# LSTM gates in the order i, f, g, o, with the output gate's columns transposed, summed and put through tanh in a later piece

## The chip, the cores and the metric

The kernel runs on one core of a Trainium2 chip. The metric is the device time of one execution in microseconds (us), less is better. A core has five engines that matter here: TensorE (PE in the profile, PEld for its weight loads) multiplies matrices into PSUM; VectorE (DVE) does elementwise work, sums along a row and transposes of 32x32 blocks; ScalarE (ACT) does tanh and copies; GpSimd (POOL) and SyncE (SP) issue transfers and little else in this kernel. Each engine works through its own list of instructions in order[...].

## The reference, cut to what matters

Four residual layers follow each other over x of shape (4, 1024, 512): a tanh RNN, a state-space layer, an LSTM and an adapted linear layer. The change touches the LSTM alone.

```python
# x = x + RNN(x, cond); x = x + SSM(x, ...); then the LSTM, width 512, 1024 steps, batch 4:
xW = jnp.einsum('ntd,dg->ntg', x, Wx) + b
c0 = jnp.zeros_like(h0)
def step(carry, xw_t):
    prev_h, prev_c = carry
    A = xw_t + prev_h @ Wh                 # (4, 2048): gates i, f, o, g
    i = jax.nn.sigmoid(A[:, 0:Hdim])
    f = jax.nn.sigmoid(A[:, Hdim:2 * Hdim])
    o = jax.nn.sigmoid(A[:, 2 * Hdim:3 * Hdim])
    g = jnp.tanh(A[:, 3 * Hdim:4 * Hdim])
    next_c = f * prev_c + i * g
    next_h = o * jnp.tanh(next_c)
    return ((next_h, next_c), next_h)
_, hs = jax.lax.scan(step, (h0, c0), jnp.swapaxes(xW, 0, 1))
# x = x + hs; then the adapted linear layer
```

Each of the 1024 steps needs the h of the step before, so no two steps of a recurrence can be computed at once. The products i*g and f*c need three gates; the output gate o is needed only when h is formed.

## The kernel before, in words

**Stages.** The sequence is cut into 32 chunks of 32 steps. A loop of passes (`do_pass`, L737) handles one chunk of the LSTM per pass, step by step (L765), and beside each LSTM step one step of the RNN, which runs 56 steps ahead (LEAD). The other layers' work for neighbouring chunks (input projections, the state-space layer, the adapted layer of the last chunk) is a list of jobs, each with a step and a place in it: "pe" after the LSTM's matmuls, "gap" in the middle of VectorE's LSTM work, "end" after the RNN's. In passes -2 and -1 only the RNN and the setup run; there Wh2 is split into three bf16 parts (`split_wh2`, L269), and Wx2, b2 and the adapted layer's weights are made ready. In pass 0 and 1 the adapted layer's matrices are also computed.

**Order.** It is written out by hand: each engine runs its instructions in the order in which the code emits them (manual schedule), and the framework only adds the semaphores that data dependences need.

**One LSTM step.** h is held as three parts of bf16 precision (`split`, L189, twice per half after h itself), so the weights loaded into TensorE are 128x12: three parts of four batch rows. The hidden units are worked in two halves, A and Bh, each of 256 units. `lstm_mm(c, t, kh, mh, ks)` (L359) emits the matmuls that take the h of half kh into the accumulator of half mh (`acc2[mh]`, a PSUM tile of 128x256): for each of two blocks k of 128 units and each of three parts n of Wh2 four matmuls, which write the four 32-row strips of the tile. A step has thus 96 matmuls, 24 groups of four. Their order (L770 to L774): A's h into A (6 groups), first block of A's h into Bh (3), Bh's h into A (6), second block of A's h into Bh (3), Bh's h into Bh (6). After the fifteenth group A's accumulator is complete.

The columns of `acc2` are four gates of 64 columns, in the reference's order i, f, o, g. `Half` (L378) has the steps that follow, for each half: `transpose` (L386, VectorE) turns the accumulator to units by batch, into `tt2`, where `lstm_input` (L375, ScalarE) has laid the input's part beside the three partial results; `sum` (L391) adds the four; `gates` (L398, ScalarE) takes tanh of all gates at once (sigmoid is written as tanh of half the value, and g's weights are doubled); `products` (L402), `cell` (L407), `tanh` (L412, ScalarE), `h` (L415) and `split` twice (L191). The tile `gc` keeps i, f, o, g and, as a fifth block, the cell state that came from the step before. The loop body from L780 interleaves the halves by hand: A's transpose and sum, Bh's transpose, A's gates, products and cell, Bh's sum, A's tanh, h and first split, Bh's gates and products, A's second split, Bh's cell; then the "gap" jobs, the copies of the next input, Bh's tanh, h and splits; then the RNN's transpose (L352), add (L353) and tanh (L356), and the "end" jobs.

The next step's first LSTM matmul reads all three parts of A's h and so waits for A's second split; its tenth group is the first that reads Bh's.

**Gates' places elsewhere.** `wx2` (L164) holds Wx2 as it lies in memory, loaded by four transfers on SP's queue; `b2` (L148) is loaded gate by gate; `split_wh2` writes the columns of gate g; `double_g` (L265) and a job at L670 double the columns and bias of g.

Of the kernel before, what the change touches and what calls it, by code (L numbers as in the profile page):

```python
# [8 lines left out]
F32 = mybir.dt.float32  # L9
BF16 = mybir.dt.bfloat16  # L10
AF = mybir.ActivationFunctionType
ALU = mybir.AluOpType
PSUM = bass.MemoryType.PSUM

P = 128
B, T, D = 4, 1024, 512
KC = D // P
TC = 32
# [4 lines left out]
CT = 32  # L23
TAPS = B
NG = 4 * KC
NS = 64
RANK = 8
WR = 2
W2_BUFS = 4
NP = 3  # L30
# [8 lines left out]
def cond_resid_kernel(ctx: ExitStack, tc: tile.TileContext, a: dict, out: bass.AP):  # L39
# [28 lines left out]
    nc = tc.nc  # L68
    ctx.enter_context(tc.manual_schedule())

    const = ctx.enter_context(tc.tile_pool(name="const", bufs=1))
# [10 lines left out]
    def quads(eng, dst, src):  # L82

        for j in range(4):
            eng.dma_start(out=dst[CT * j : CT * (j + 1)], in_=src[j])

    def load_rows(pool, name, src, n, eng):

        t = pool.tile([P, KC, n], F32, name=name, tag=name)
        quads(eng, t, src.rearrange("(j c q) n -> j q c n", j=4, c=KC))  # L90
        return t
# [21 lines left out]
    gc = [turns(4, f"gc{m}", [P, 5, 2, B]) for m in range(2)]  # L113
    prod = [turns(2, f"prod{m}", [P, 2, 2, B]) for m in range(2)]
# [4 lines left out]
    x1 = state.tile([P, KC, 3 + TC, B], F32, name="x1", tag="x1")  # L119
    s1 = state.tile([NS, B], F32, name="s1", tag="s1")  # L120

# [25 lines left out]
    bo = load_vec(const, "bo", a["bo"].rearrange("j (c q) -> j q c", q=CT).unsqueeze(2), 1, nc.gpsimd)  # L147
    b2 = const.tile([P, 4, KC], F32, name="b2", tag="b2")  # L148
    for g in range(4):
        quads(nc.gpsimd, b2[:, g], a["b2"].rearrange("(g j) (c q) -> g j q c", g=4, q=CT)[g])  # L150

    load_x(1, a["xT"][1])
    load_x(2, a["xT"][2])
# [1 line left out]
    layer = const.tile([P, B, KC, D], F32, name="layer", tag="layer")  # L155
    for c in (1, 0, 2, 3):
        quads(nc.sync, layer[:, c], a["Wh2"].rearrange("(j c q) (g n) -> j c q g n", j=4, c=KC, g=4)[:, c])
    wh2 = [const.tile([P, KC, 4 * D], BF16, name=f"wh2{i}", tag=f"wh2{i}") for i in range(NP)]
# [2 lines left out]
    quads(nc.sync, wp[:, TAPS - 1], a["Wp"].rearrange("(j c q) n -> j q c n", j=4, c=KC))  # L161
    ws = load_rows(const, "ws", a["Ws"], NS, nc.sync)
    wo = load(const, "wo", [NS, D], a["Wo"], nc.sync)
    wx2 = load_rows(const, "wx2", a["Wx2"], 4 * D, nc.sync)  # L164
    w1 = layer[:, 1]

    base = layer[:, B - 1]
# [17 lines left out]
    def upper(x):  # L185

        return x.bitcast(BF16)[..., 1::2]
# [12 lines left out]
    for n in range(1, NP):  # L200
        split(h2[1][:, :, TC - 1], n)
    for m in range(2):
        nc.vector.memset(gc[m][0][:, 4], 0.0)
    nc.vector.memset(x1[:, :, 0:3, :], 0.0)
    nc.vector.memset(s1, 0.0)

# [1 line left out]
    acc2 = [psum.tile([P, 2 * P], F32, name=f"acc2{i}", tag=f"acc2{i}") for i in range(2)]  # L208
# [54 lines left out]
                nc.gpsimd.tensor_scalar(wp[:, tap, k], whole[:, k], condT[:, k, tap : tap + 1], None, ALU.mult)  # L263

    def double_g(k):  # L265
        w = wx2[:, k, 3 * D :]
        nc.scalar.activation(w, w, AF.Copy, scale=2.0)

    def split_wh2(k, g):  # L269

        w, scale, cols = layer[:, k, g], 1.0 if g == 3 else 0.5, slice(g * D, (g + 1) * D)
        part = [x[:, k, cols] for x in wh2]
        left = xw2[1][:, 2 + g % 2].rearrange("p c t b -> p (c t b)")

        def first():
            nc.scalar.activation(part[0], upper(w), AF.Copy, scale=scale)
            nc.vector.scalar_tensor_tensor(left, w, scale, part[0], ALU.mult, ALU.subtract)

        def second():
            nc.scalar.copy(part[1], upper(left))  # L280
            nc.vector.tensor_tensor(part[2], left, part[1], ALU.subtract)

        return first, second
# [72 lines left out]
        nc.scalar.activation(h0[c % 2][:, :, t, :], pre0[t % 2], AF.Tanh)  # L356


    def lstm_mm(c, t, kh, mh, ks=(0, 1)):  # L359


        h = h2[c % 2] if t else h2[(c - 1) % 2]
        for k in (2 * kh + x for x in ks):
            parts = upper(h[:, k, (t - 1) % TC].rearrange("p s b -> p (s b)"))
            for n in range(NP):
                w = wh2[n][:, k].rearrange("p (g n) -> p g n", g=4)
                for j in range(4):
                    n0 = P * j + 2 * CT * mh
                    nc.tensor.matmul(  # L369
                        acc2[mh][CT * j : CT * j + NP * B, :], parts, w[:, :, n0 : n0 + 2 * CT],  # L370
                        start=(k == 0 and n == 0), stop=(k == KC - 1 and n == NP - 1),
                    )

    def lstm_input(c, t, m):
        nc.scalar.copy(tt2[m][t % 2][:, :, :, :B], xw2[c % 2][:, :, 2 * m : 2 * m + 2, t, :])  # L375
# [1 line left out]
    class Half:  # L377


        def __init__(self, c, t, m):  # L380
            self.m, self.tt, self.gc, self.th = m, tt2[m][t % 2], gc[m][t % 4], th2[m][t % 4]
            self.prod, self.c = prod[m][t % 2], gc[m][(t + 1) % 4][:, 4]
            self.out = h2[c % 2][:, 2 * m : 2 * m + 2, t]

        def transpose(self):
            nc.vector.transpose(  # L386
                self.tt[:, :, :, B:].rearrange("p g c b -> p (g c) b"), acc2[self.m]
            )

        def sum(self):  # L390
            nc.vector.tensor_reduce(  # L391
                self.gc[:, :4].rearrange("p g c b -> p (g c) b"),
                self.tt[:, :, :, : (1 + NP) * B].rearrange("p g c (s b) -> p (g c) b s", b=B),
                axis=mybir.AxisListType.X, op=ALU.add,
            )

        def gates(self):
            nc.scalar.activation(self.gc[:, :4], self.gc[:, :4], AF.Tanh, scale=0.5)  # L398

        def products(self):  # L400

            nc.vector.scalar_tensor_tensor(  # L402
                self.prod, self.gc[:, 0:2], 1.0, self.gc[:, 3:5], ALU.add, ALU.mult
            )

        def cell(self):
# [6 lines left out]

        def h(self):
            nc.vector.scalar_tensor_tensor(  # L415
                self.out[:, :, 0], self.gc[:, 2], 1.0, self.th, ALU.add, ALU.mult
            )

        def split(self, n):
# [222 lines left out]
    def at(c, t, f):  # L642
        early.setdefault((c, t), []).append(f)

    def at_step(i, f):

        c, t = divmod(i - LEAD, TC)
        at(c, t, f)
# [18 lines left out]
    at_step(25, adapt_norm)  # L667
    for half in range(2):
        at_step(26 + half, lambda half=half: adapt_bias(half))
    at_step(26, lambda: nc.scalar.activation(b2[:, 3], b2[:, 3], AF.Copy, scale=2.0))  # L670
    for k in range(KC):
        at_step(27 + k, lambda k=k: double_g(k))
    at_step(31, adapt_hidden)
# [12 lines left out]
    for n in range(B * KC):  # L686
        c, t = divmod(24 + 4 * n // 3, TC)
# [49 lines left out]
    def do_pass(c, first=0, src=None, dst=None):  # L737

        lstm = c >= 0
        jobs = []  # L740
        if dst is not None:
            jobs += adapt_jobs(c - 1, dst)
        if -1 <= c < NCHUNK - 1:
            jobs += ssm_jobs(c + 1)
            jobs += input_jobs(
                c + 1, 0, range(25, 29), ((28, "end"), (29, "gap"), (29, "end"), (30, "gap"))
            )
        if src is not None:
            jobs.append((9, "end", lambda: load_x(c + 4, src)))
        if c + 3 < NCHUNK:  # L750
            for m in range(KC):
                mm, end = project0(c + 3, m)
                t = (18, 20, 22, 30)[m]
                jobs += [(t, "pe", mm), (t, "end", end)]
        if lstm:
            jobs += input_jobs(c, 1, range(4), ((3, "end"), (4, "gap"), (4, "end"), (5, "gap")))
            jobs += input_jobs(c, 2, range(4, 8), ((8, "gap"), (8, "end"), (9, "gap"), (9, "end")))
            jobs += input_jobs(c, 3, range(9, 17, 2), ((15, "end"), (16, "gap"), (18, "gap"), (19, "gap")))

        def do(t, place):  # L760
            for slot, where, f in jobs:
                if (slot, where) == (t, place):
                    f()

        for t in range(first, TC):  # L765
            r = divmod(c * TC + t + LEAD, TC)
            rnn = r[0] < NCHUNK
            if lstm:
                A, Bh = Half(c, t, 0), Half(c, t, 1)
                lstm_mm(c, t, 0, 0)  # L770
                lstm_mm(c, t, 0, 1, (0,))
                lstm_mm(c, t, 1, 0)
                lstm_mm(c, t, 0, 1, (1,))
                lstm_mm(c, t, 1, 1)  # L774
            do(t, "pe")
            if rnn:
                rnn_mm(*r)
            if c * TC + t < 8 - TC:
                keep_busy()
            if lstm:  # L780
                A.transpose()
                A.sum()
                Bh.transpose()
                A.gates()
                A.products()
                A.cell()
                Bh.sum()
                A.tanh()
                A.h()
                A.split(1)  # L790
                Bh.gates()
                Bh.products()
                A.split(2)
                Bh.cell()
            do(t, "gap")
            if lstm:
                if (c, t) != (NCHUNK - 1, TC - 1):
                    for m in range(2):
                        lstm_input(c if t + 1 < TC else c + 1, (t + 1) % TC, m)
                Bh.tanh()  # L800
                Bh.h()
                Bh.split(1)
                Bh.split(2)
            if rnn:
                rnn_pre(*r)
                rnn_h(*r)
            do(t, "end")
            for f in early.pop((c, t), ()):
                f()
# [77 lines left out]
```

## Time and profile before

| | us |
|---|---|
| median of 3 runs | 4768.19 (4766.73 to 4770.69) |
| the profiled execution, its own time | 4770.03 |
| its span, first to last instruction | 4768.2 |
| TensorE busy (matmuls) | 4608.4 (97%) |
| TensorE weight loads | 3524.3 (74%) |
| VectorE busy | 3867.3 (81%) |
| ScalarE busy | 1493.9 (31%) |
| first and last transpose of an LSTM accumulator (L386) | 158.2 and 4755.2 |

What lies around the span is 1.8 us. The page's chain of work that ended last is followed back from the last instruction, at each step to what released it. The timeline lists instructions by time: start, duration, engine, line, operation and tiles, and in brackets how long the engine sat idle before it and what ended that. Groups of instructions give the count, the busy time in all, the mean of one in ns, and the idle time before them. Matmuls' ends are modelled: each is drawn with its latency, though four on different strips of PSUM run side by side and the next group starts before the last has ended.

### The profile page before, as it was taken

What the parts mean: (1) busy time and instruction counts of PE and PEld (TensorE: products, weight loads), DVE (VectorE), ACT (ScalarE), POOL (GpSimd) and SP (SyncE); (2) the same over time, 40 slices, a digit from 0 to 9 for tenths busy, and PEclk for the clock granted to TensorE, in tenths of its full rate; (3) what the DMA queues carried; (4) which work ended last, traced back from release to release, by engine and by line L of the source; (5) the groups of instructions that cost most, each with busy time, mean ns of one, the idle gap of its engine ahead of it and who ended that gap; (6) DMA issues with size and microseconds to landing.
All of it is one profiled execution on the core that took longest, in us unless ns stands there. A gap on an engine that the chain in (4) does not pass through costs nothing.

```text
span 4768.2 us, 320158 instructions
## 1 busy us (share of the span) xinstructions
PE 4608.4 (97%) x146784; PEld 3524.3 (74%) x146784; DVE 3867.3 (81%) x18001; ACT 1493.9 (31%) x7645; POOL 45.6 (1%) x80
## 2 busy tenths in 40 slices
PE   7999999999999999999999999999999999999976
PEld 5767777777777777777777777777777777777654
DVE  3688888888888888888888888888888888888876
ACT  2223333333333333333333333333333333333322
POOL 3000000000000000000000000000000000000000
PEclk9999999999999999999999999999999999999999
DMA  6300000000000000000000000000000000000000
GB/s 148 112 13 9 9 7 9 9 7 9 9 7 9 9 7 9 9 7 9 9 7 9 9 7 9 9 7 9 9 7 9 9 7 9 9 5 7 6 5 7
DMA packets 38266, 67.36 MB, mean 14 GB/s; under 512 B 8609, under 2 KB 25505, under 8 KB 35889
## 3 DMA queue, kind: packets, MB, share of 16 engines
q1 hardware_dynamic: 34064, 46.68, 3.6%
q8 instruction: 1147, 18.79, 1.6%
q14 instruction: 207, 1.69, 0.1%
q0 software_dynamic: 1696, 0.19, 0.0%
q10 hardware_dynamic: 1152, 0.01, 0.0%
HBM read 38.34 MB, written 8.39 MB: 10 GB/s over the span
## 4 chain that ended last, share of the span: by engine, by line
PE 94%; DVE 4%; DMA 1%; issue 1%; ACT 0%; SPq 0%; ACTq 0%; DVEq 0%
PE acc L369 59%; PE acc L337 18%; PE proj L318 9%; PE pb L292 3%; PE proj L292 2%; PE ada L703 2%; DVE tt L386 1%; DVE gc L391 1%; DVE h L191 1%; PE ssm_out L292 1%; DMA layer<-in_w_dram 1%; DVE h L415 0%; DVE prod L402 0%; DVE gc L407 0%; PE pl L625 0%
## 5 line engine op out<-in xcount | busy, mean ns | idle before, releaser
L369 PE MATMUL acc<-wh,h 128*12 128x256 bf16 x98304 | 2868.0, 273 | 118.4 <-DVE h L191 115.2
L369 PEld LDWEIGHTS <-h 128*12 128x12 bf16 x98304 | 2262.6, 87 | 676.8 <-DVE h L191 360.6
L386 DVE STREAM_TRANSPOSE tt<-acc 128x256 f32<-128x256 f32 x2048 | 920.9, 450 | 429.2 <-PE acc L369 301.4
L337 PEld LDWEIGHTS acc<-wh,h 128*4 128x4 f32 x32768 | 805.4, 87 | 510.0 <-issue 214.8
L337 PE MATMUL acc<-wh,h 128*4 128x128 f32 x32768 | 1086.1, 273 | 18.1 <-ACT h L356 11.0
L398 ACT ACTIVATE gc<-gc 128x32 f32<-128x32 f32 x2048 | 469.8, 229 | 1279.1 <-DVE gc L391 1192.2
L391 DVE TENSOR_REDUCE gc<-tt 128x32 f32<-128x128 f32 x2048 | 775.4, 379 | 35.3
L191 DVE TENSOR_TENSOR h<-h 128x8 f32<-128x8 f32 (+1 forms) x4098 | 680.5, 166 | 104.8
L412 ACT ACTIVATE th<-gc 128x8 f32<-128x8 f32 x2048 | 427.7, 209 | 830.1 <-DVE gc L407 830.1
L356 ACT ACTIVATE h<-pre 128x16 f32<-128x16 f32 x1024 | 221.2, 216 | 1132.2 <-DVE pre L353 1132.2
L318 PE MATMUL proj<-wx,x 128*32 128x512 f32 x4096 | 529.1, 592 | 1.1 <-DVE x L507 1.1
L415 DVE SCALAR_TENSOR_TENSOR h<-gc,th 128x8 f32<-128x8 f32 x2048 | 341.8, 167 | 144.6 <-ACT th L412 134.7
L407 DVE SCALAR_TENSOR_TENSOR gc<-prod 128x8 f32<-128x8 f32 x2048 | 342.0, 167 | 35.5
L352 DVE STREAM_TRANSPOSE tt<-acc 128x128 f32<-128x128 f32 x1024 | 316.0, 309 | 61.8 <-PE acc L337 61.6
L375 ACT COPY tt<-xw 128x32 f32<-128x32 f32 x2048 | 327.8, 207 | 0.0
L402 DVE SCALAR_TENSOR_TENSOR prod<-gc 128x16 f32<-128x16 f32 x2048 | 314.3, 153 | 0.0
L353 DVE TENSOR_TENSOR pre<-xw,tt 128x16 f32<-128x16 f32 x1024 | 179.3, 175 | 38.0 <-DVE tt L352 0.5
L292 PE MATMUL proj<-xin,wx 128*32 128x128 f32 x4096 | 137.9, 278 | 11.1 <-DMA wx<-in_Wx_dram 11.1
L703 PE MATMUL ada<-layer,x 128*32 128x512 f32 x1024 | 133.9, 599 | 3.0 <-DVE x L696 3.0
L292 PE MATMUL pb<-x,wp 128*32 128x128 f32 x4096 | 134.4, 273 | 0.0
L292 PEld LDWEIGHTS proj<-xin,wx 128*32 128x32 f32 x4096 | 117.5, 112 | 14.9 <-DMA wh<-in_Wh_dram 11.1
L318 PEld LDWEIGHTS proj<-wx,x 128*32 128x32 f32 x4096 | 118.3, 110 | 6.6 <-DVE x L507 1.4
(118 smaller groups left out, 1168.8 us busy)
## 6 DMA issues: line engine op xcount, KB each, us to landing
layer<-in_w2T_dram SPq DMA_DIRECT2D x32, 512.0 KB, 4.5
xin<-in_xT_dram SPq DMA_DIRECT2D x128, 64.0 KB, 2.4
out_dram<-x SPq DMA_DIRECT2D x128, 64.0 KB, 2.0
layer<-in_Wh_dram SPq DMA_DIRECT2D x16, 256.0 KB, 9.9
wx<-in_Wx_dram SPq DMA_DIRECT2D x4, 1024.0 KB, 15.6
wx<-in_Wx_dram SPq DMA_DIRECT2D x4, 256.0 KB, 4.6
wh<-in_Wh_dram SPq DMA_DIRECT2D x4, 256.0 KB, 7.2
layer<-in_w_dram SPq DMA_DIRECT2D x4, 256.0 KB, 23.9
```

Source lines behind the costliest of these rows:

```text
L191: nc.vector.tensor_tensor(h[:, :, n], h[:, :, n - 1], upper(h[:, :, n - 1]), ALU.subtract)
L292: nc.tensor.matmul(dst[CT * j : CT * (j + 1)], columns(j), x, start=first, stop=final)
L318: nc.tensor.matmul(ps[CT * j : CT * (j + 1), :], tok, w[:, j], start=(k == 0), stop=(k == KC - 1))
L337: nc.tensor.matmul(acc0[CT * j : CT * j + B, :], h[:, k, (t - 1) % TC, :], wh0[:, k, j * P : (j + 1) * P], start=(k == 0), stop=(k == KC - 1),
L369: nc.tensor.matmul(acc2[mh][CT * j : CT * j + NP * B, :], parts, w[:, :, n0 : n0 + 2 * CT], start=(k == 0 and n == 0), stop=(k == KC - 1 a ...
L375: nc.scalar.copy(tt2[m][t % 2][:, :, :, :B], xw2[c % 2][:, :, 2 * m : 2 * m + 2, t, :])
L386: nc.vector.transpose(self.tt[:, :, :, B:].rearrange("p g c b -> p (g c) b"), acc2[self.m])
L391: nc.vector.tensor_reduce(self.gc[:, :4].rearrange("p g c b -> p (g c) b"), self.tt[:, :, :, : (1 + NP) * B].rearrange("p g c (s b) -> p ( ...
L398: nc.scalar.activation(self.gc[:, :4], self.gc[:, :4], AF.Tanh, scale=0.5)
L407: nc.vector.scalar_tensor_tensor(self.c, self.prod[:, 1], 0.5, self.prod[:, 0], ALU.mult, ALU.add)
L412: nc.scalar.activation(self.th, self.c, AF.Tanh, scale=0.5)
L415: nc.vector.scalar_tensor_tensor(self.out[:, :, 0], self.gc[:, 2], 1.0, self.th, ALU.add, ALU.mult)
```

## The change

The gates are kept in the order i, f, g, o in all places (`PLACE` maps the old place to the new one): in b2, in the columns of the split Wh2, in Wx2 and in `gc`, where the cell state now lies fourth and the output gate fifth. Wx2's load becomes three slices of columns, each by four transfers. For each half, the transpose, the sum and tanh are each cut in two: the first piece takes i, f and g (192 of the 256 columns, 24 of the 32 gate columns after the sum), the second the output gate (64 and 8). A's second pieces of transpose and sum stand right behind its first; Bh's are spread among A's later steps, and Bh's first transpose now stands between A's products and A's cell. `lstm_mm` takes a list of the six (k, n) groups instead of blocks k, and one group moves: Bh's accumulator gets two groups before Bh's h is read and four after A is complete, instead of three and three.

```diff
+PLACE = (0, 1, 3, 2)
...
-        quads(nc.gpsimd, b2[:, g], a["b2"].rearrange("(g j) (c q) -> g j q c", g=4, q=CT)[g])
+        quads(nc.gpsimd, b2[:, PLACE[g]], a["b2"].rearrange("(g j) (c q) -> g j q c", g=4, q=CT)[g])
...
-    wx2 = load_rows(const, "wx2", a["Wx2"], 4 * D, nc.sync)
+    wx2 = const.tile([P, KC, 4 * D], F32, name="wx2", tag="wx2")
+    for src, dst, n in ((0, 0, 2), (3, 2, 1), (2, 3, 1)):
+        quads(
+            nc.sync, wx2[:, :, dst * D : (dst + n) * D],
+            a["Wx2"].rearrange("(j c q) n -> j q c n", j=4, c=KC)[:, :, :, src * D : (src + n) * D],
+        )
...
-    def lstm_mm(c, t, kh, mh, ks=(0, 1)):
+    def lstm_mm(c, t, kh, mh, parts=range(2 * NP)):
...
+        for x in parts:
+            k, n = 2 * kh + x // NP, x % NP
+            w = wh2[n][:, k].rearrange("p (g n) -> p g n", g=4)
+            for j in range(4):
...
-        def transpose(self):
+        def transpose(self, g0=0, g1=3):
             nc.vector.transpose(
-                self.tt[:, :, :, B:].rearrange("p g c b -> p (g c) b"), acc2[self.m]
-            )
-
-        def sum(self):
+                self.tt[:, g0:g1, :, B:].rearrange("p g c b -> p (g c) b"),
+                acc2[self.m][:, 2 * CT * g0 : 2 * CT * g1],
+            )
+
+        def sum(self, g0=0, g1=3, to=0):
             nc.vector.tensor_reduce(
-                self.gc[:, :4].rearrange("p g c b -> p (g c) b"),
-                self.tt[:, :, :, : (1 + NP) * B].rearrange("p g c (s b) -> p (g c) b s", b=B),
+                self.gc[:, to : to + g1 - g0].rearrange("p g c b -> p (g c) b"),
+                self.tt[:, g0:g1, :, : (1 + NP) * B].rearrange("p g c (s b) -> p (g c) b s", b=B),
                 axis=mybir.AxisListType.X, op=ALU.add,
             )
 
-        def gates(self):
-            nc.scalar.activation(self.gc[:, :4], self.gc[:, :4], AF.Tanh, scale=0.5)
+        def gates(self, g0=0, g1=3):
+            nc.scalar.activation(self.gc[:, g0:g1], self.gc[:, g0:g1], AF.Tanh, scale=0.5)
+
+        def transpose_o(self):
+            self.transpose(3, 4)
+
+        def sum_o(self):
+            self.sum(3, 4, to=4)
+
+        def gate_o(self):
+            self.gates(4, 5)
 
         def products(self):
             nc.vector.scalar_tensor_tensor(
-                self.prod, self.gc[:, 0:2], 1.0, self.gc[:, 3:5], ALU.add, ALU.mult
+                self.prod, self.gc[:, 0:2], 1.0, self.gc[:, 2:4], ALU.add, ALU.mult
             )
...
                 lstm_mm(c, t, 0, 0)
-                lstm_mm(c, t, 0, 1, (0,))
+                lstm_mm(c, t, 0, 1, (0, 1))
                 lstm_mm(c, t, 1, 0)
-                lstm_mm(c, t, 0, 1, (1,))
+                lstm_mm(c, t, 0, 1, (2, 3, 4, 5))
                 lstm_mm(c, t, 1, 1)
...
                 A.transpose()
                 A.sum()
-                Bh.transpose()
+                A.transpose_o()
+                A.sum_o()
                 A.gates()
                 A.products()
+                A.gate_o()
+                Bh.transpose()
                 A.cell()
+                Bh.transpose_o()
+                A.tanh()
                 Bh.sum()
-                A.tanh()
+                Bh.gates()
                 A.h()
+                Bh.sum_o()
                 A.split(1)
-                Bh.gates()
+                Bh.gate_o()
                 Bh.products()
                 A.split(2)
                 Bh.cell()
             do(t, "gap")
```

`h` reads the output gate from `gc[:, 4]` instead of `gc[:, 2]`; `double_g`, `split_wh2` and the job that doubles b2's g use the new places.

More of the change, by code (lines that the diff above doesn't have):

```diff
@@ L202, in cond_resid_kernel @@
     for m in range(2):
-        nc.vector.memset(gc[m][0][:, 4], 0.0)
+        nc.vector.memset(gc[m][0][:, 3], 0.0)
     nc.vector.memset(x1[:, :, 0:3, :], 0.0)
@@ L265, in double_g @@
     def double_g(k):
-        w = wx2[:, k, 3 * D :]
+        w = wx2[:, k, 2 * D : 3 * D]
         nc.scalar.activation(w, w, AF.Copy, scale=2.0)
     def split_wh2(k, g):
-        w, scale, cols = layer[:, k, g], 1.0 if g == 3 else 0.5, slice(g * D, (g + 1) * D)
+        w, scale, cols = layer[:, k, g], 1.0 if g == 3 else 0.5, slice(PLACE[g] * D, (PLACE[g] + 1) * D)
         part = [x[:, k, cols] for x in wh2]
@@ L356, in rnn_h @@
         nc.scalar.activation(h0[c % 2][:, :, t, :], pre0[t % 2], AF.Tanh)
-    def lstm_mm(c, t, kh, mh, ks=(0, 1)):
+    def lstm_mm(c, t, kh, mh, parts=range(2 * NP)):
         h = h2[c % 2] if t else h2[(c - 1) % 2]
[L363 to L371, printed above, removed]
-                    )
+        for x in parts:
+            k, n = 2 * kh + x // NP, x % NP
+            w = wh2[n][:, k].rearrange("p (g n) -> p g n", g=4)
+            for j in range(4):
+                n0 = P * j + 2 * CT * mh
+                nc.tensor.matmul(
+                    acc2[mh][CT * j : CT * j + NP * B, :],
+                    upper(h[:, k, (t - 1) % TC].rearrange("p s b -> p (s b)")), w[:, :, n0 : n0 + 2 * CT],
+                    start=(k == 0 and n == 0), stop=(k == KC - 1 and n == NP - 1),
+                )
     def lstm_input(c, t, m):
@@ L381, in __init__ @@
             self.m, self.tt, self.gc, self.th = m, tt2[m][t % 2], gc[m][t % 4], th2[m][t % 4]
-            self.prod, self.c = prod[m][t % 2], gc[m][(t + 1) % 4][:, 4]
+            self.prod, self.c = prod[m][t % 2], gc[m][(t + 1) % 4][:, 3]
             self.out = h2[c % 2][:, 2 * m : 2 * m + 2, t]
-        def transpose(self):
+        def transpose(self, g0=0, g1=3):
             nc.vector.transpose(
-                self.tt[:, :, :, B:].rearrange("p g c b -> p (g c) b"), acc2[self.m]
+                self.tt[:, g0:g1, :, B:].rearrange("p g c b -> p (g c) b"),
+                acc2[self.m][:, 2 * CT * g0 : 2 * CT * g1],
             )
-        def sum(self):
+        def sum(self, g0=0, g1=3, to=0):
             nc.vector.tensor_reduce(
-                self.gc[:, :4].rearrange("p g c b -> p (g c) b"),
-                self.tt[:, :, :, : (1 + NP) * B].rearrange("p g c (s b) -> p (g c) b s", b=B),
+                self.gc[:, to : to + g1 - g0].rearrange("p g c b -> p (g c) b"),
+                self.tt[:, g0:g1, :, : (1 + NP) * B].rearrange("p g c (s b) -> p (g c) b s", b=B),
                 axis=mybir.AxisListType.X, op=ALU.add,
             )
-        def gates(self):
-            nc.scalar.activation(self.gc[:, :4], self.gc[:, :4], AF.Tanh, scale=0.5)
+        def gates(self, g0=0, g1=3):
[6 more added lines that the diff above has]
+            self.gates(4, 5)
         def products(self):
             nc.vector.scalar_tensor_tensor(
-                self.prod, self.gc[:, 0:2], 1.0, self.gc[:, 3:5], ALU.add, ALU.mult
+                self.prod, self.gc[:, 0:2], 1.0, self.gc[:, 2:4], ALU.add, ALU.mult
             )
@@ L415, in h @@
             nc.vector.scalar_tensor_tensor(
-                self.out[:, :, 0], self.gc[:, 2], 1.0, self.th, ALU.add, ALU.mult
+                self.out[:, :, 0], self.gc[:, 4], 1.0, self.th, ALU.add, ALU.mult
             )
@@ L669, in cond_resid_kernel @@
         at_step(26 + half, lambda half=half: adapt_bias(half))
-    at_step(26, lambda: nc.scalar.activation(b2[:, 3], b2[:, 3], AF.Copy, scale=2.0))
+    at_step(26, lambda: nc.scalar.activation(b2[:, 2], b2[:, 2], AF.Copy, scale=2.0))
     for k in range(KC):
```

## The prediction

> **What bounds the kernel now.** I read the page from the top, and its chain first. By it the kernel is bound by TensorE:
>
> ```profile
> PE 94%; DVE 4%; DMA 1%; issue 1%; ACT 0%; SPq 0%; ACTq 0%; DVEq 0%
> ```
>
> That can't be taken as it stands, since ends of matmuls are modelled (each is drawn 273 ns long, and four run side by side). So I went to the timeline, one LSTM step in the middle (start, duration, engine, line, tile, in us):
>
> ```profile
> 2507.50 2.80 PE L369 MATMUL acc<-wh,h 128*12 128x256 bf16 x96
> ...
> 2509.37 0.45 DVE L386 STREAM_TRANSPOSE tt<-acc 128x256 f32<-128x256 f32 x1
> ...
> 2509.85 0.39 DVE L391 TENSOR_REDUCE gc<-tt 128x32 f32<-128x128 f32 x1
> ...
> 2510.12 1.05 PE L292 MATMUL pb<-x,wp 128*32 128x128 f32 x32
> 2510.28 0.23 ACT L398 ACTIVATE gc<-gc 128x32 f32<-128x32 f32 x1 [1.19 <-DVE gc L391]
> 2510.35 0.45 DVE L386 STREAM_TRANSPOSE tt<-acc 128x256 f32<-128x256 f32 x1
> 2510.72 0.13 DVE L402 SCALAR_TENSOR_TENSOR prod<-gc 128x16 f32<-128x16 f32 x1
> 2510.89 0.17 DVE L407 SCALAR_TENSOR_TENSOR gc<-prod 128x8 f32<-128x8 f32 x1
> ...
> 2510.97 0.37 DVE L391 TENSOR_REDUCE gc<-tt 128x32 f32<-128x128 f32 x1
> ...
> 2511.74 0.17 DVE L191 TENSOR_TENSOR h<-h 128x8 f32<-128x8 f32 x1
> 2511.85 0.17 DVE L407 SCALAR_TENSOR_TENSOR gc<-prod 128x8 f32<-128x8 f32 x1
> ...
> 2511.95 2.50 PEld L369 LDWEIGHTS <-h 128*12 128x12 bf16 x96 [0.20 <-DVE h L191]
> ...
> 2512.50 0.37 DVE L191 TENSOR_TENSOR h<-h 128x8 f32<-128x8 f32 x2
> ```
>
> The 96 LSTM matmuls start at 2507.50 and the next job's at 2510.12: 24 groups of four, 0.109 us a group. A group starts 0.34 before VectorE may transpose what it completes (B: group 24 at 2510.01, transpose at 2510.35). Half A is complete with group 15 (2509.03), and its transpose starts at 2509.37. From there the A chain runs to its second split, 2511.74+0.17 = 2511.91, and 0.04 to 0.05 later the weights of the next step are loaded. So there is a loop: 1.87 from first matmul to transpose, 2.58 back. That is 4.455, and the A transposes of the same view stand at 2500.46, 2504.91, 2509.37, 2513.82 and 2518.28, 4.455 apart. TensorE itself needs 24+8+8 groups, 4.36, in a step that has a job beside LSTM and RNN. A second loop is nearly as long: B's last split ends at 2512.87 and, 0.055 later, its weights serve group 10, which is due at 2511.96+9x0.109 = 2512.94. It has 0.015 to spare. Thus any step's time is the later of loop A and loop B; 960 of 1024 steps (passes 2 to 31) run at about 4.46.
>
> [...] 8 columns cost 167 ns (L407), 224 only 388. Cutting in two therefore costs. [...] which way the sum's 380 ns divides no row shows, and this decides the case.
>
> **The change, part by part.** Prices first. Groups of instructions of one pass (142.75 us; after the count busy us, mean ns of one, idle before it):
>
> ```profile
> L386 DVE STREAM_TRANSPOSE tt<-acc 128x256 f32<-128x256 f32 x64 | 28.8, 450 | 11.8 <-PE acc L369 7.7
> L391 DVE TENSOR_REDUCE gc<-tt 128x32 f32<-128x128 f32 x64 | 24.3, 380 | 1.1
> L352 DVE STREAM_TRANSPOSE tt<-acc 128x128 f32<-128x128 f32 x32 | 9.9, 308 | 0.0
> L696 DVE SCALAR_TENSOR_TENSOR x<-h,x 128x128 f32<-128x128 f32 x4 | 1.5, 381 | 0.0
> ```
>
> Transposes: 308 at 128 columns and 450 at 256, so 35.5 per 32 columns: 380 for three gates (192), 238 for one (64). A pair costs 618 where 450 stood. Sums: L434 takes 388 at 224 columns and 226 at 64, so a plain instruction is 161 + 1.01 per element. The sum is 380 at 128, 90 more. If the extra goes with elements (1.71 each) the pieces are 325 (96 elements) and 216 (32). If it is fixed they are 348 and 283. Below the first pair nothing in the page points; with no fixed share of 161 at all they'd be 285 and 95, which every small row excludes. I take 325/216, since L696 has the same extra on 128 elements that it writes far apart and is no sum. tanh: 229 at 32 columns, 209 at 8: 222 and 209.
>
> Queue rules, from the timeline: an instruction that needs its predecessor starts 0.035 after its end; one that needs nothing 0.08 before it; from or to ScalarE 0.03 to 0.035.
>
> One step of the new order, us from A's transpose (ATo, ASo: the output gate's piece), old start beside it:
>
> ```
>          dur   old   new  new start set by
> A  T     .380  0     0    TensorE
> A  S     .325  .48   .415 T
> A  To    .238   -    .66  queue
> A  So    .216   -    .93  To
> A  prod  .133  1.35  1.07 queue (tanh ends 1.00)
> B  T     .380  .98   1.12 queue (TensorE: 1.09)
> A  cell  .167  1.52  1.41 queue
> B  To    .238   -    1.50 queue
> B  S     .325  1.60  1.66 queue
> A  h     .167  1.96  1.90 queue (tanh ends 1.82)
> B  So    .216   -    1.98 queue
> A  split .167  2.16  2.12 queue
> B  prod  .175  2.27  2.27 tanh, 2.015 to 2.24
> A  split .165  2.37  2.36 queue
> B  cell  .167  2.48  2.48 B prod
> B  h     .167  2.93  2.92 tanh, 2.68 to 2.89
> B  splits      3.13  3.13 end 3.49 (old 3.50)
> ```
>
> So about 0.44 more of VectorE's queue fits where it waited: 0.11 for TensorE before B's transpose, and A's products no longer stand behind that transpose. Loop A: second split ends 2.53, +0.055, then A is complete with group 14, since one group of B's has moved behind it: 13x0.109+0.34 = 1.76; together 4.34. Loop B: 3.49+0.055, then A's six last groups, 5x0.109+0.34 = 0.885; together 4.43. Loop B decides: 4.43 against 4.455, 0.025 a step. Moving the group is worth nothing beside loop B, but without it B's weights, ready at 3.55, would wait for group 10's turn (2.585+0.98 = 3.57).
>
> The rest costs nothing, and this covers it. The two more tanh instructions (209 each): ScalarE's next is A's tanh at 1.62, when the first has ended at 1.39; the second ends at 2.44, and behind it stand the two copies of L375 (0.32) and B's tanh, due 2.68. Without that cover up to 0.1 would be added. B's transpose now stands before A's cell and waits for TensorE, with 0.03 to spare; were it late, all below it would be too. End and gap jobs: RNN's add ends at 3.93, two end jobs of 0.28 at 4.34 at the latest, before 4.43. Setup: Wx2's load becomes 12 issues on SP's queue instead of 4, eight more of 0.56 (4 in 2.25 at 41.9 us), 4.5 us; its first reader is at 93.7, and the loads of w1 and w2 behind it are used later still. Renamed columns of b2, Wh2 and gc move no work.
>
> Sum: 960 steps and about half of the first 64 (the others are held at 5.2 to 5.5 by TensorE's jobs of the last layer), 990x0.025 = 25 us. From the profiled execution, 4770.0 (span 4768.2), that is 4745; the runs' median is 1.8 lower, so **4743**.
>
> **Rivals.**
> *Slower: a fixed price of the second sum.* With 348/283 the column above grows by twice the first piece's excess and once the second's, 2x23+67 = 113 ns: 4.54 a step, +0.088x990 = 87, 4855. It decides from the point where twice the first piece plus the second passes 866+25 = 891 ns. For it: the small-instruction rows. Against: L696. Between the ends (333/240) a step is 4.47 and the time 4783.
> *No change.* B's cell and splits come out where they were (2.48 in both columns); a transpose piece of 250 instead of 238 adds 0.03 and cancels the gain: 4768, within 0.2%, which is about what a measurement of this kernel can tell from no change.
> *TensorE takes over.* If pieces cost less than I take, or VectorE's products are shorter behind a transpose (0.13 against 0.17), the floor is TensorE's 4.36 plus 0.02 where weights change: 4.38, 990x0.075 = 74 less, 4694. It can't get better in steps with a job.
>
> **How the numbers follow.** Faster by loop B as worked out, 0.45, own range 4715 to 4758; TensorE's floor or near it, 0.10; no change, 0.12; slower by the sums, 0.33. Faster by over 0.2%: 0.55; within: 0.12; slower: 0.33. For 8 in 10 the range leaves out half of the floor's cases below 4702 and the dearest of the slower ones above 4845.
>
> **What would show it.** In the profile after: L386's and L391's successors in two forms, 380/238 and 325/216; A transposes 4.43 apart; weight loads of LSTM waiting for a split once in mid-step (B's), TensorE idle there some 0.07; A's products at 1.07. Wrong if the sum of one gate takes over 240, if B's transpose starts after 1.12 for TensorE, or if B's tanh waits behind copies.

## The result, and the profile after

The changed kernel takes 4698.16 us (median of 4 runs, 4696.22 to 4701.41) against 4767.46 us before (4 runs): a ratio of 0.9853, 95% interval 0.9839 to 0.9867, so 69 us or 1.5% faster. The forecast was 4743 us, in the right direction and too small by a factor of nearly three; the measured time is 4 us below the range.

First the groups of instructions of the changed kernel in 140.41 us, the length of one pass (142.75 before). They answer the price rows of before; after the count: busy us, mean ns of one, idle time before it.

```profile
L393 DVE STREAM_TRANSPOSE tt<-acc 128x192 f32<-128x192 f32 x65 | 24.6, 379 | 7.6 <-PE acc L374 6.8
L399 DVE TENSOR_REDUCE gc<-tt 128x24 f32<-128x96 f32 x64 | 19.5, 304 | 1.1
L393 DVE STREAM_TRANSPOSE tt<-acc 128x64 f32<-128x64 f32 x64 | 15.2, 238 | 0.0
L399 DVE TENSOR_REDUCE gc<-tt 128x8 f32<-128x32 f32 x64 | 13.1, 205 | 1.1
L406 ACT ACTIVATE gc<-gc 128x24 f32<-128x24 f32 x64 | 14.3, 223 | 34.6 <-DVE gc L399 34.5
```

The prices were 380, 325, 238, 216 and 222. Only the sums are cheaper, on average. Then the timeline of the changed kernel, one step in the middle (start, duration, engine, line, operation, tiles; the step's A transpose is the first line, the next step's the last):

```profile
2504.11 0.38 DVE L393 STREAM_TRANSPOSE tt<-acc 128x192 f32<-128x192 f32 x1 [0.50 <-PE acc L374]
2504.52 0.33 DVE L399 TENSOR_REDUCE gc<-tt 128x24 f32<-128x96 f32 x1
2504.77 0.24 DVE L393 STREAM_TRANSPOSE tt<-acc 128x64 f32<-128x64 f32 x1
...
2504.89 0.22 ACT L406 ACTIVATE gc<-gc 128x24 f32<-128x24 f32 x1 [0.53 <-DVE gc L399]
...
2505.05 0.21 DVE L399 TENSOR_REDUCE gc<-tt 128x8 f32<-128x32 f32 x1
2505.18 0.16 DVE L419 SCALAR_TENSOR_TENSOR prod<-gc 128x16 f32<-128x16 f32 x1
2505.26 0.37 DVE L393 STREAM_TRANSPOSE tt<-acc 128x192 f32<-128x192 f32 x1
...
2505.60 0.24 DVE L393 STREAM_TRANSPOSE tt<-acc 128x64 f32<-128x64 f32 x1
...
2505.77 0.28 DVE L399 TENSOR_REDUCE gc<-tt 128x24 f32<-128x96 f32 x1
...
2506.55 0.17 DVE L424 SCALAR_TENSOR_TENSOR gc<-prod 128x8 f32<-128x8 f32 x1
2506.64 0.81 PEld L374 LDWEIGHTS <-h 128*12 128x12 bf16 x32
2506.70 2.83 PE L374 MATMUL acc<-wh,h 128*12 128x256 bf16 x96
...
2507.19 0.37 DVE L197 TENSOR_TENSOR h<-h 128x8 f32<-128x8 f32 x2
...
2507.61 1.63 PEld L374 LDWEIGHTS <-h 128*12 128x12 bf16 x64 [0.15 <-DVE h L197]
...
2508.49 0.38 DVE L393 STREAM_TRANSPOSE tt<-acc 128x192 f32<-128x192 f32 x1
```

The reader is to see four things. A's transposes are 4.38 apart (2504.11, 2508.49). A's products start 1.07 after A's transpose, where they started 1.35 after it before, and nothing in VectorE's list from there to B's cell (2506.55) waits for TensorE. The weight loads of the LSTM now stop once in the middle: 32 of 96 are done by 2507.45, the other 64 start at 2507.61, 0.05 after B's last split ended (2507.56). And the sum of three gates takes 0.33 for A, where it waited for its transpose, and 0.28 for B, where it did not wait and stood right behind a transpose of another gate.

By the starts of A's transpose over passes 4 to 30, a step went from 4.455 to 4.380 us (medians; by their place in a pass the steps lie between 4.374 and 4.396, but for step 24, which takes 4.61 in both kernels). Thirty passes at 2.33 us less are 70 us. The span fell by 73.8 us, 2.0 of which lie ahead of the first LSTM step. Medians below are over the same passes, without step 24.

### The profile page after: what moved, and what is told of

It reads as the page before. It is cut to its first block, busy times and chain, and to the rows that moved or that the text cites. A ratio compares the mean times of both kernels' runs of the same rounds, so it can differ in the third digit from the quotient of the medians.

```text
span 4694.4 us, 326310 instructions
## 1 busy us (share of the span) xinstructions
PE 4551.9 (97%) x146784; PEld 3575.0 (76%) x146784; DVE 3950.4 (84%) x22097; ACT 1877.0 (40%) x9693; POOL 45.1 (1%) x80
## 4 chain that ended last, share of the span: by engine, by line
PE 90%; DVE 7%; DMA 1%; issue 1%; ACT 0%; SPq 0%; DVEq 0%; ACTq 0%
PE acc L374 55%; PE acc L343 18%; PE proj L324 9%; PE pb L298 3%; DVE tt L393 3%; DVE gc L399 2%; PE ada L720 2%; PE proj L298 2%; DVE prod L419 1%; PE ssm_out L298 1%; DVE h L197 1%; DMA layer<-in_Wh_dram 0%; PE pl L642 0%; DMA wx<-in_Wx_dram 0%; PE pp L606 0%
## 5 line engine op out<-in xcount | busy, mean ns | idle before, releaser
L374 PE MATMUL acc<-wh,h 128*12 128x256 bf16 x98304 | 2903.0, 273 | 100.2 <-DVE h L197 94.9
L374 PEld LDWEIGHTS <-h 128*12 128x12 bf16 x98304 | 2313.9, 87 | 556.1 <-DVE h L197 181.0
L393 DVE STREAM_TRANSPOSE tt<-acc 128x192 f32<-128x192 f32 (+1 forms) x4096 | 1233.7, 309 | 298.5 <-PE acc L374 274.5
L406 ACT ACTIVATE gc<-gc 128x24 f32<-128x24 f32 (+1 forms) x4096 | 855.2, 216 | 1399.4 <-DVE gc L399 1391.4
L343 PE MATMUL acc<-wh,h 128*4 128x128 f32 x32768 | 1085.5, 273 | 17.5 <-ACT h L362 11.6
L399 DVE TENSOR_REDUCE gc<-tt 128x24 f32<-128x96 f32 (+1 forms) x4096 | 1037.6, 255 | 70.5
L197 DVE TENSOR_TENSOR h<-h 128x8 f32<-128x8 f32 (+1 forms) x4098 | 671.1, 164 | 69.9
L432 DVE SCALAR_TENSOR_TENSOR h<-gc,th 128x8 f32<-128x8 f32 x2048 | 328.3, 160 | 144.2 <-ACT th L429 134.5
L419 DVE SCALAR_TENSOR_TENSOR prod<-gc 128x16 f32<-128x16 f32 x2048 | 347.5, 170 | 13.0
L424 DVE SCALAR_TENSOR_TENSOR gc<-prod 128x8 f32<-128x8 f32 x2048 | 297.2, 145 | 0.0
```

The costliest lines, as they stand in the source:

```text
L197: nc.vector.tensor_tensor(h[:, :, n], h[:, :, n - 1], upper(h[:, :, n - 1]), ALU.subtract)
L343: nc.tensor.matmul(acc0[CT * j : CT * j + B, :], h[:, k, (t - 1) % TC, :], wh0[:, k, j * P : (j + 1) * P], start=(k == 0), stop=(k == KC - 1),
L374: nc.tensor.matmul(acc2[mh][CT * j : CT * j + NP * B, :], upper(h[:, k, (t - 1) % TC].rearrange("p s b -> p (s b)")), w[:, :, n0 : n0 + 2 ...
L393: nc.vector.transpose(self.tt[:, g0:g1, :, B:].rearrange("p g c b -> p (g c) b"), acc2[self.m][:, 2 * CT * g0 : 2 * CT * g1],)
L399: nc.vector.tensor_reduce(self.gc[:, to : to + g1 - g0].rearrange("p g c b -> p (g c) b"), self.tt[:, g0:g1, :, : (1 + NP) * B].rearrange( ...
L406: nc.scalar.activation(self.gc[:, g0:g1], self.gc[:, g0:g1], AF.Tanh, scale=0.5)
```

## The experiments

Theory Q: each step is set by the later of two loops, one through half A and one through half B, and what sets these is the order in VectorE's list; after the change it is loop B. Rival P: TensorE with its 40 groups of matmuls (4.36 us) has become the bound, and the moved group did it. It deserved a hearing, since the forecast gave 4694 us for it. A third: A's earlier tanh is the gain. Each ratio below is to runs of the kernel before on the same chip.

**The moved group alone.**

```diff
 # the kernel before
-                lstm_mm(c, t, 0, 1, (0,))
+                lstm_mm(c, t, 0, 1, (0, 1))        # two groups of B ahead
                 lstm_mm(c, t, 1, 0)
-                lstm_mm(c, t, 0, 1, (1,))
+                lstm_mm(c, t, 0, 1, (2, 3, 4, 5))  # four behind
```

> The kernel before with nothing but the moved group of matmuls (two groups for B before B's h is read, four after A is complete). Theory Q (the step is set by the loop through B's half, and by what stands in VectorE's queue): B's accumulator comes a group (0.11 us) later beside A's, B's transpose stands ahead of A's products and waits for it, so both halves are late: a step of 4.54 us, in all some 4850 us, slower than before. Rival P (the bound after the change is TensorE's 40 groups, and the order of its matmuls brought the gain): near 4700 us. If the move is worth what it saves in loop A alone: 4.42 us a step, 4732 us.

Measured: 4852.31 us, ratio 1.0182 (1.0166 to 1.0197). Slower by nearly 2%, as theory Q has it, and against rival P. Its timeline shows how a move on TensorE that brings A forward makes A later (same columns; 0.22 idle for TensorE where it was 0.11, and the products behind it):

```profile
2503.09 0.45 DVE L386 STREAM_TRANSPOSE tt<-acc 128x256 f32<-128x256 f32 x1 [0.17 <-PE acc L368]
2503.58 0.38 DVE L391 TENSOR_REDUCE gc<-tt 128x32 f32<-128x128 f32 x1
...
2503.99 0.23 ACT L398 ACTIVATE gc<-gc 128x32 f32<-128x32 f32 x1 [1.15 <-DVE gc L391]
2504.18 0.45 DVE L386 STREAM_TRANSPOSE tt<-acc 128x256 f32<-128x256 f32 x1 [0.22 <-PE acc L368]
2504.56 0.13 DVE L402 SCALAR_TENSOR_TENSOR prod<-gc 128x16 f32<-128x16 f32 x1
```

A's tanh ends at 2504.22, but B's transpose, 1.09 after A's instead of 0.98, stands ahead of A's products, which start at 1.47 instead of 1.35.

**The moved group taken back.**

```diff
 # the changed kernel
-                lstm_mm(c, t, 0, 1, (0, 1))
+                lstm_mm(c, t, 0, 1, (0, 1, 2))
                 lstm_mm(c, t, 1, 0)
-                lstm_mm(c, t, 0, 1, (2, 3, 4, 5))
+                lstm_mm(c, t, 0, 1, (3, 4, 5))
```

> The changed kernel with the matmuls' groups as they were (three and three). Theory Q: group 10 is due a group later, 0.09 us after the first step's start, which is 0.01 us later than B's weights are ready: a step of 4.39 us instead of 4.38, in all 4705 to 4712 us. Rival P: the move was the gain, so 4765 us.

Measured: 4713.09 us, ratio 0.9887 (0.9873 to 0.9902), a step of 4.397, just above the expected range. So the move is worth 0.3% in the changed kernel and costs 1.8% in the old one: the pieces, not TensorE's order, bring the gain. The forecast was right that B's weights would otherwise wait for their turn: here they are used 0.072 us after B's last split, where 0.054 is enough in the changed kernel. Since that turn is counted from the step's first matmul, which waits for A's last split, the bound without the move is loop A again (A's last split at 2.476, 0.056 to the first matmul, 1.865 to the next transpose: 4.397).

**Order alone.** The kernel before, whole pieces.

```diff
 # the kernel before
                 A.transpose()
                 A.sum()
-                Bh.transpose()
                 A.gates()
                 A.products()
+                Bh.transpose()
                 A.cell()
```

> The kernel before with whole pieces and gates in their old order, and B's transpose behind A's products instead of ahead of them. Theory Q: VectorE now waits for A's tanh with nothing to fill the wait, A's products come 0.19 us earlier and B's transpose 0.26 us later: a step of 4.56 us, in all some 4870 us. A rival, that the order brings the gain and the cut only pays for it: faster than before, near 4700 us.

Measured: 4894.93 us, ratio 1.0259 (1.0243 to 1.0274), 4.59 us a step. With B's transpose out of the way A's products wait for A's tanh, and there is nothing for VectorE to do meanwhile (timeline; in brackets the idle time):

```profile
2506.07 0.38 DVE L391 TENSOR_REDUCE gc<-tt 128x32 f32<-128x128 f32 x1
...
2506.48 0.23 ACT L398 ACTIVATE gc<-gc 128x32 f32<-128x32 f32 x1 [1.16 <-DVE gc L391]
2506.74 0.17 DVE L402 SCALAR_TENSOR_TENSOR prod<-gc 128x16 f32<-128x16 f32 x1 [0.30 <-ACT gc L398]
...
2506.84 0.44 DVE L386 STREAM_TRANSPOSE tt<-acc 128x256 f32<-128x256 f32 x1
```

The 0.30 is the hole that the output gate's transpose and sum fill in the changed kernel. The new order and the moved group together, with whole pieces, were not run. An estimate from this run: B's last split ends at 3.638 and the changed kernel takes 0.937 from there to A's transpose, so 4.57 us a step, still slower than before.

**One half in pieces.** For both, gates in the new order, the cell state one block further on; the first keeps the moved group and has B whole at the places of B's first pieces, the second has A whole, B's first transpose ahead of A's products, and three groups and three.

```diff
 # the changed kernel, only A in pieces
-                Bh.transpose()
+                Bh.transpose(0, 4)
                 A.cell()
-                Bh.transpose_o()
                 A.tanh()
-                Bh.sum()
-                Bh.gates()
+                Bh.sum(0, 4)
+                Bh.gates(0, 4)
                 A.h()
-                Bh.sum_o()
                 A.split(1)
-                Bh.gate_o()
                 Bh.products()
```

> The changed kernel with only A in two pieces; B's transpose, sum and tanh are whole, at the places of their first pieces. (The cell state lies one block further on, and the products read g and c two blocks apart.) Theory Q: B's whole transpose and sum take 0.12 us longer until B's tanh may start, less what the second pieces took of the queue; a step of 4.45 us, in all 4755 to 4770 us: no gain left. A rival, that A's half brings the gain since its tanh starts earlier: 4698 us.

```diff
 # the changed kernel, only B in pieces
-                A.transpose()
-                A.sum()
-                A.transpose_o()
-                A.sum_o()
-                A.gates()
+                A.transpose(0, 4)
+                A.sum(0, 4)
+                Bh.transpose()
+                A.gates(0, 4)
                 A.products()
-                A.gate_o()
-                Bh.transpose()
                 A.cell()
```

> Only B in two pieces, A whole, B's first transpose ahead of A's products as before, groups three and three as before. Theory Q: loop B falls to 4.42 us, but A's chain stays nearly as it was, 4.43 to 4.45 us a step: 4745 to 4765 us. The rival that A brings the gain: 4768 us or more.

Measured: A alone 4771.45 us, ratio 0.9997 (0.9988 to 1.0006); B alone 4767.73 us, ratio 0.9992 (0.9984 to 1.0001), both slightly above the time that theory Q gave; the kernel before took 4771.65 us on that chip. Both run at some 4.455 us a step. With A alone in pieces loop B is as long as loop A was before: B's last split ends at 3.52 after A's transpose, against 3.44 with both halves in pieces. With B alone loop A is what it was, with A's last split ending at 2.54, and loop B fell less than was expected (4.44 by this run's figures, not 4.42). Cutting one half gains nothing measurable, and the third theory falls with it: with A alone in pieces A's tanh starts as early as in the changed kernel. Both kernels also carry the renamed columns and the twelve loads of Wx2, which therefore cost nothing that shows.

**B's tanh later.**

```diff
 # the changed kernel; spare is a tile of 128x16
+                for _ in range(2):
+                    nc.scalar.copy(spare[:, :8], spare[:, 8:])
                 Bh.tanh()
```

> The changed kernel with two spare copies of 8 columns on ScalarE ahead of B's second tanh; the first fits into its wait, the second delays it by some 0.09 us. Only B's h is later by this, A's chain of the same step is done. Theory Q: the whole delay shows in each step, 4.46 to 4.47 us, in all 4780 to 4795 us. Rival P, or a theory in which loop A is the bound (0.09 us shorter than loop B by my reading): 4698 to 4705 us.

Measured: 4880.48 us, ratio 1.0238 (1.0222 to 1.0253): 182 us above the changed kernel, twice what was expected. The size of the delay was misjudged, not its effect. The timeline of this run:

```profile
2505.93 0.42 ACT L826 COPY spare<-spare 128x8 f32<-128x8 f32 x2
...
2506.26 0.20 ACT L431 ACTIVATE th<-gc 128x8 f32<-128x8 f32 x1
2506.50 0.17 DVE L434 SCALAR_TENSOR_TENSOR h<-gc,th 128x8 f32<-128x8 f32 x1 [0.46 <-ACT th L431]
...
2507.12 1.63 PEld L376 LDWEIGHTS <-h 128*12 128x12 bf16 x64 [0.34 <-DVE h L199]
```

The two copies, which write the same place, took 0.42 one after the other, where the two copies of the next input overlap and take 0.32. What makes the difference was not tried apart. B's h came 0.195 later (3.070 after A's transpose instead of 2.875, medians), the weight loads waited 0.34 for it instead of 0.15, and the step grew by the same 0.195, from 4.380 to 4.575. Over thirty passes of 31 such steps that is 181 us of the 182. A delay of B alone shows in full, so loop B is the bound after the change. Neither TensorE nor loop A is, in the steps other than the 24th.

**The output gate turned first.**

```diff
 # the changed kernel
                 A.transpose()
-                A.sum()
                 A.transpose_o()
+                A.sum()
                 A.sum_o()
```

> The changed kernel with A's second transpose ahead of A's first sum, nothing else. Theory Q: the second transpose starts 0.08 us before the first ends and so fills the wait that the sum had, the second sum no longer waits for its transpose, loop B falls to 4.33 us, and TensorE's 40 groups (4.364 us) become the bound in steps that have a job; the two steps of a pass without one go at 4.33 us. In all 4682 us (4675 to 4690). Rival P (TensorE is already the bound): no change, 4698 us. A theory in which A's tanh is what counts (it starts 0.04 us later here): 4735 us.

Measured: 4679.91 us, ratio 0.9818 (0.9801 to 0.9834), the fastest of all, 18 us below the changed kernel. Groups of this kernel in 140 us:

```profile
L399 DVE TENSOR_REDUCE gc<-tt 128x24 f32<-128x96 f32 x64 | 18.8, 294 | 0.0
L393 DVE STREAM_TRANSPOSE tt<-acc 128x64 f32<-128x64 f32 x64 | 14.2, 222 | 0.0
L399 DVE TENSOR_REDUCE gc<-tt 128x8 f32<-128x32 f32 x64 | 12.8, 199 | 0.0
L419 DVE SCALAR_TENSOR_TENSOR prod<-gc 128x16 f32<-128x16 f32 x64 | 11.2, 175 | 5.9 <-ACT gc L406 5.5
```

The sums' waits are gone (0.0 where it was 1.1), each of the three pieces in the first rows is shorter than in the changed kernel, and the products wait for tanh instead of for the queue. A's products start at 1.03, B's last split ends at 3.42, and the median step is 4.36. A's tanh starts no later than in the changed kernel (0.04 later was expected), so this run says nothing on the third theory. The two steps without a job were expected at 4.33 and take 4.354 and 4.357, so loop B fell only to 4.36. In steps with a job TensorE hardly waits for B's weights any more (median 0.002 us, mean 0.010, where the changed kernel has 0.024 and 0.027). TensorE's own work, some 4.355 us, and loop B are thus equally long here, and what else could be won on VectorE is small as long as TensorE's work stays.

## Why the prediction was wrong

**The bound before, and the mechanism: right.** Two loops through VectorE's list, TensorE near but not at its limit; the second pieces fill VectorE's waits; loop B decides after the change. The runs in which one part was taken away or delayed agree. The moved group is worth little, and only beside the pieces: right, and the price of having it without them (B's transpose ahead of A's products) was not foreseen in the prediction. TensorE's busy share of the whole span, 97%, comes near the 98% that 4.36 us needed of 4.455 make, but that does not hold step by step: over one step of the trace before (2506.92 to 2511.38) the matmuls are drawn busy for all of its 4.46 us, and there the busy share hides TensorE's wait.

**The size: wrong.** The forecast step was 4.43 and the measured one 4.380, a gain of 0.075 instead of 0.025. By the prediction's own column (us from A's transpose; medians):

| | forecast | measured |
|---|---|---|
| A's products, start and duration | 1.07, .133 | 1.061, .164 |
| B's transpose | 1.12 | 1.143 |
| A's cell, start and duration | 1.41, .167 | 1.443, .123 |
| B's sum, start | 1.66 | 1.651 |
| B's sum, duration | .325 | .284 |
| B's products | 2.27 | 2.224 |
| B's cell | 2.48 | 2.434 |
| B's last split, end | 3.49 | 3.443 |
| split to matmul, and six groups to A's transpose | .940 | .937 |
| the step | 4.43 | 4.380 |

The term that failed is the row "B S .325", the price of B's sum. B's tanh, products and cell hang from the end of this sum. It was priced as A's, which waits for its transpose. Standing in the queue behind the transpose of another gate it took 0.284, so 0.041 less, and it started 0.009 earlier. That is the 0.05 by which the forecast step was too long; all rows below only carry it on, and the way through TensorE was right. In this column an error of 0.04 in one instruction is more than the whole gain forecast. Two other rows were priced wrongly for the same reason and nearly cancel: A's products took more, since they no longer stand behind a transpose, and A's cell took less, since it now does. That is luck. Over some 960 steps (step 24 of each pass gains nothing) 0.05 is 48 us, and the forecast lacks 45.

The slack of loop B before was nearly right: 0.021, where the prediction had 0.015. That the sum's 380 ns divide by elements (325 and 216 taken, 325 and 210 measured where the sum waits) was the decision the prediction feared most, and it held: the slower rival did not come.

**The rival at 4694 us** met the time to 4 us, but by coincidence. Its place was TensorE. In the changed kernel TensorE waits for B's weights in steps with a job (0.024 us; the prediction had some 0.07) and longer, 0.09, in the two steps without one, and yet these are as long (4.377 and 4.378 against 4.380). A delay of B alone shows in full, and another order on VectorE alone gains 18 us more. TensorE's own work is 0.02 short of the step, which is how near the two bounds lie. The 0.02 that the rival added to 4.36 where weights change was an estimate, which the traces do not show: in the changed kernel 0.099 us pass from the LSTM's last matmul to a job's first and from the RNN's last to the LSTM's first (medians, outside step 24), as between two groups of the LSTM. The rival's condition, that pieces cost less than taken, did come true. Its other one, products shorter behind a transpose, did not, for they came to stand behind a sum; but a shorter row behind a transpose is what B's sum and A's cell have.

**The covers held**, with one size off: the first tanh piece's successor came when it was done, B's transpose did not wait for TensorE (1.09 against a start at 1.143), the end jobs fit. B's tanh did not wait for the two copies: they end when B's cell does, within 0.02 us, and tanh starts 0.033 after the cell, as it did before. Wx2's twelve issues took 13.8 us on SP's queue instead of 2.25, not 4.5 more but 11.6; the first reader, at 91.8, did not wait.

## What to carry to other kernels

When two chains share an engine and each is nearly the step's length, write down the engine's list with start and cause of each instruction, and give both chains their slack: a change to one half or to one engine's order can gain nothing, or lose, where both together gain (here ratios of 0.9997 and 0.9992, 1.0182 and 1.0259, against 0.9853). Cutting a transpose and a sum in two cost VectorE time (transposes of 379 and 238 ns where one took 450, sums of 304 and 205 where one took 380), but paid here because the second pieces fell into waits that the first ones' results caused. Where the gain hangs on hundredths of a us, a price belongs to an instruction together with what stands ahead of it (the sum of three gates: 325 ns after a wait, 284 behind a transpose): take it from a place in the list like the one where it will stand, and where there is none, give the price a range.

## What the runs showed of the hardware

In these kernels the length of a VectorE instruction's row went with what stood directly ahead of it (medians; the start is some 75 ns before the end of the one ahead, unless it waits).

| | after a wait | behind a transpose of an LSTM accumulator | behind another instruction |
|---|---|---|---|
| sum of three gates | 325 ns | 304 (A's, output gate turned first), 282 to 286 (B's) | - |
| products | 175 | 132 | 164 (a sum) |
| cell | 167 | 123 to 125 | 167 (a split) |
| sum of one gate | 210 | - | 199 to 201 (a sum or h) |
| transpose of the output gate | - | 207 | 236 to 242 (a sum or a cell) |

So the marked effect, 20 to 45 ns, is that of such a transpose ahead; a queue alone gives little or nothing. The run with the output gate turned first shows it on one and the same instruction, A's sum, by order alone. In all of these kernels an instruction that needs nothing from the one ahead starts 74 to 84 ns before the end of its row if nothing else holds it, and one that needs its result 34 ns after. Why the rows are shorter, and why A's sum and B's differ behind the same transpose, the runs do not show.

Step 24 of each pass took some 4.605 us in the kernel before, in the changed one and in all seven others, also in those whose other steps took 4.36 or 4.59. No order on VectorE moved it, for in this step TensorE's own list is the bound: the next step's first matmul starts 0.08 to 0.40 us after A's last split, where 0.055 is enough, and B's first group follows without a wait. The step's job is the output of the state-space layer, 32 matmuls of 64 rows, and TensorE lets 0.20 us pass from the matmul ahead to its first, where 0.10 pass before every other job, and 0.20 again from its last to the next matmul. Why it does so was not tried.
